# Moments of attention rows on ScalarE, the scan's skip term on TensorE, and a re-paced start of the experts in a fused state-space, attention and mixture-of-experts kernel

## The chip, the cores and the metric

The kernel runs on one core of a Trainium2 chip. The metric is the device time of one execution in microseconds. Before the change, three runs took 3665.78, 3655.67 and 3658.45 us; the median is 3658.45 us. One more execution was recorded with the hardware profiler.

## The reference

The input is four images of 384 channels and 32 x 32 places (1,024 tokens each), float32 throughout. Two layers follow each other:

```python
# layer 0: a selective scan over four directions k, 16 states n, after a group norm u = gn(x)
dt = softplus(dts + dt_bias)
h = h * exp(dt * A) + (dt * u) * B        # step by step along the 1,024 places
y = sum_n h * C  (+ Ds * u)               # summed over the four directions
x = x + gelu(layernorm_c(y) * ln_w + ln_b)
# layer 1, on tokens t = x transposed
t = t + softmax(causal(q k^T * scale)) v  # q, k, v from ln(t)
t = t + sum over the 2 best of 4 experts of  p_e * (gelu(ln(t) w1_e + b1_e) w2_e + b2_e)
```

`Ds * u` is the skip term. `ln(t)` in front of the experts needs the mean and the variance of each attention output row of 384 numbers.

## The kernel before

**The scan.** The work of layer 0 is cut into 768 units: 4 images x 3 channel blocks m of 128 x 4 directions x 16 units of 128 partitions (32 channels x 4 states) by 1,024 places. For a unit, `decay` (ScalarE) makes `da = exp(dt * a)`, `front` (VectorE, L709) the product `v = du * B` into PSUM, `middle` (VectorE, L715) the scan `h` from `da` and `v`, `back` (GpSimd, L732) the product of `h` with C. After every four units, `row` (L757) has TensorE sum the states of four h tiles into `y`, a PSUM tile of one block of channels. In the first image part of the `v` comes from TensorE and ScalarE instead (`feed`, `turned`). h has seven buffers; `ahead` makes VectorE wait, at each fourth unit, until the row sums of the four units before are done.

**Planner.** The program is written out by a loop over ticks `t`, one unit per tick. In every tick it emits the scan's instructions and then lets other work go on, which is written as generators: `preparation` of the next image, and on the list `waiting` the attention and the experts of the image before. A generator yields `("wait", n)`, to be taken up again n ticks later, or `("pe", x)`, which charges x us of TensorE to the budget of the tick: `PACE_A` 4.4 in attention, `PACE_E` 3.1 in the experts. All engines run their instructions in the order in which this loop emits them. `defer(n, f)` emits f n ticks later. `slots` are eight shared SBUF buffers, `banks` the shared PSUM banks; both are given back in the planner's time, and semaphores hold the engines to it. What is left after the last unit, the attention and experts of the fourth image (`alone`), runs by itself.

**Around the change.** `skip` (L765) loads `xe`, the normalised input of a block, when the last direction begins; `evict` (L773), two ticks after the last row sum of the block, adds `dsum * xe` to `y` and writes `yb` (L777); with the third block the image's layer norm begins (`finish`). In `attention`, `values` (L1225) sums an output row block of 128 tokens into the bank `po`; its inner `rows` (L1240) takes the moments with two VectorE instructions (L1242, L1243), copies the rows to `yb` on ScalarE and gives the bank back. `ready` (L1296) turns moments into `rstd` and `shift` and normalises the rows. `chosen` (L1368) ranks the experts, places the tokens, and sends each row block with two indirect DMAs of GpSimd's queue to its places in `xsd` (`scatter`, L1491); it adds to `routed` when they are emitted. `experts` (L1604) waits for all of `routed` (L1835), loads the first 256 rows (`load(0)`), turns them with TensorE, and goes through 11 blocks: `first_` (L1720) is 6 steps of 2 x 3 matmuls of w1 tiles (L1740), `second_` (L1774) 6 steps of matmuls of w2 tiles (L1790). Each step charges `PART` = 2.6 us (x `STEP`, which is 3 in the last image). `need` and `weights` fetch the weight tiles (384 KB each) up to four ahead. Blocks are filled by the data: `by_rows` branches to 256, 128 or no rows.

Of the kernel before, what the change touches and what calls it, by code (L numbers as in the profile page):

```python
# [9 lines left out]
F32 = mybir.dt.float32  # L10
# [7 lines left out]
P = 128  # L18
# [29 lines left out]
PACE_E = 3.1  # L48
PACE_T = 1.5
PART = 2.6  # L50
BT = 256
LIMIT = 44.0
EDGE = 40.0
# [5 lines left out]
def hybrid_kernel(  # L59
# [131 lines left out]
    def act(dst, src, f, **more):  # L191

        if f in KINDS:
            tables_for(KINDS[f])
        return nc.scalar.activation(dst, src, f, **more)  # L195
# [569 lines left out]
    def skip(b, m):  # L765
        xe = yield from slots.take(f"xe_{b}_{m}", P, L)
        nc.sync.dma_start(xe, xn_d[b][:, m, :])
        xes[b, m] = xe

    ybs = {}  # L770
    held = []
# [1 line left out]
    def evict(b, m):  # L773
        if m == 0:
            assert not held, f"tick {clock[0]}: the image before still needs the buffer"
            ybs[b] = one.tile([P, M, L], F32, tag="yb", name=f"yb_{b}")
        nc.vector.scalar_tensor_tensor(  # L777
            ybs[b][:, m, :], xes[b, m], dsum[:, m : m + 1], ys[b, m], ALU.mult, ALU.add
        )
        slots.give(f"xe_{b}_{m}")  # L780
        if m == M - 1:
            held.append(b)
            side.append(finish(b))
            waiting.append(behind(b))
# [322 lines left out]
    def attention(b, yb, fx0):  # L1107
# [117 lines left out]
        def values(i):  # L1225
            name = f"po_{b}_{i}"
            po = yield from banks.take(name)
            s = bass.ts(i, P)
            for m in range(M):
                nc.tensor.matmul(  # L1230
                    po[:, m * P : (m + 1) * P], yb[:, m, s], ident, start=(m == 0), stop=False
                )
            for j in range(i + 1):
                nc.tensor.matmul(  # L1234
                    po[:, :C], pts[i][:, j, :], vt[:, j, :], start=False, stop=(j == i)
                )
            yield "pe", 1.2 + 0.65 * (i + 1)
            slots.give(f"pt_{b}_{i}")

            def rows():  # L1240
                stat = sm.tile([P, 6], F32, tag="stat", name=f"stat_{b}_{i}")
                nc.vector.bn_stats(stat, po[:, :C])  # L1242
                nc.vector.bn_aggr(moments[:, i, :], stat)  # L1243
                nc.scalar.copy(yb[:, :, s], po[:, :C].rearrange("p (m t) -> p m t", m=M))
                banks.give(name)

                def kept():
                    nc.sync.dma_start(
                        t2_d[b][s, :].rearrange("p (m t) -> p m t", m=M), yb[:, :, s]
                    )  # L1250

                if alone:
                    kept()
                else:
                    defer(2, kept)
                for h, (q0, n) in enumerate(GROUPS):
                    if i == q0 + n - 1:
                        defer(1, lambda h=h, q0=q0, n=n: side.append(
                            ready(b, h, yb, group_rows(q0, n), moments)
                        ))  # L1260

            defer(1, rows, inner)
# [33 lines left out]
    def ready(b, h, yb, rows, moments):  # L1296

        alone = b == B - 1
        name = f"{b}_{h}"
        q0, n = GROUPS[h]  # L1300
        mean = moments[:, q0 : q0 + n, 0]
        rstd = small("rstd", name, 1, n)[:, 0, :]
        shift = small("shift", name, 1, n)[:, 0, :]
        act(rstd, moments[:, q0 : q0 + n, 1], AF.Sqrt, bias=eps)
        yield "wait", 1
        nc.vector.reciprocal(rstd, rstd)
        nc.vector.scalar_tensor_tensor(shift, mean, -1.0, rstd, ALU.mult, ALU.mult)
        yield "wait", 1
        for q in range(n):
            act(  # L1310
                rows[q].rearrange("p (m t) -> p m t", m=M), yb[:, :, bass.ts(q0 + q, P)],
                AF.Identity, bias=shift[:, q : q + 1], scale=rstd[:, q : q + 1],
            )
            if q % 2:
                yield "wait", 1
        if h == LAST:
            held.clear()
        xts = {}
        for q in range(n):
            if q % 2 == 0:  # L1320
                xt = yield from slots.take(f"xt_{name}_{q}", P, 2, C)
            ps = yield from banks.take(f"pxt_{name}_{q}")
            for m in range(M):
                nc.tensor.transpose(
                    ps[:, m * P : (m + 1) * P], rows[q][:, m * P : (m + 1) * P], ident
                )
            yield "pe", 0.5

            def put(q=q, ps=ps, xt=xt):
                nc.scalar.copy(xt[:, q % 2, :], ps[:, :C])  # L1330
                banks.give(f"pxt_{name}_{q}")
                xts[q] = xt[:, q % 2, :]

            defer(1, put)
        while len(xts) < n:
            yield "wait", 1
        yield "wait", 1
        pg = yield from banks.take(f"pgate_{name}")
        for q in range(n):
            for c in range(M):  # L1340
                nc.tensor.matmul(
                    pg[:, q * E : (q + 1) * E], xts[q][:, c * P : (c + 1) * P], gw[:, c, :],
                    start=(c == 0), stop=(c == M - 1),
                )
        if h == LAST:
            gated.add(b)
        yield "pe", 0.65 * n
        slots.give(*[f"xt_{name}_{q}" for q in range(0, n, 2)])
        yield "wait", 1
        groups = GROUPS if alone else WIDE  # L1350
        g = [i for i, (g0, gn) in enumerate(groups) if g0 <= q0 < g0 + gn][0]
        g0, gn = groups[g]
        if (b, g) not in raw:
            raw[b, g] = small("sc", f"{b}_{g}", gn, E), []
        sc, whole = raw[b, g]
        nc.vector.tensor_tensor(
            sc[:, q0 - g0 : q0 - g0 + n], pg[:, : n * E].rearrange("p (q e) -> p q e", e=E),
            gb.unsqueeze(1).to_broadcast([P, n, E]), ALU.add,
        )
        banks.give(f"pgate_{name}")  # L1360
        whole.extend(rows)
        if len(whole) < gn:
            return
        yield from chosen(b, g, sc, whole)
# [3 lines left out]
    def chosen(b, h, sc, rows):  # L1368
# [63 lines left out]
        cum = choice()  # L1432
        if not alone:
            slots.give(f"cmp_{name}")
        yield "wait", 1
        while h > 0 and (b, h - 1) not in counted:
            yield "wait", 1
        counted.add((b, h))
# [52 lines left out]
        def scatter(q):  # L1491
            for i in range(2):
                nc.gpsimd.indirect_dma_start(  # L1493
                    out=views[2 * (q0 + q) + i],
                    out_offset=bass.IndirectOffsetOnAxis(
                        ap=placed[:, q0 + q, i : i + 1], axis=0
                    ),
                    in_=rows[q], in_offset=None,
                )

        if alone:
            yield "wait", 1
            for q in range(n):
                scatter(q)
            routed.add((b, h))
            probabilities()
            kept()
            yield "wait", 1
        mts = []
        for part in parts:  # L1510
# [7 lines left out]
            yield "wait", 1  # L1518
            nc.scalar.copy(mt[:, : len(part) * P], pm[:E, : len(part) * P])
            banks.give(f"pm_{name}_{part[0]}")  # L1520
        if not alone:
            for q in range(n):
                scatter(q)
                if q < n - 1:
                    yield "wait", 1
            routed.add((b, h))
        nc.vector.tensor_tensor(
            two, at.unsqueeze(1).to_broadcast([P, 2, E, n]),
            spot.rearrange("p q i -> p i q").unsqueeze(2).to_broadcast([P, 2, E, n]), ALU.is_equal,
# [74 lines left out]
    def experts(b, route):  # L1604
# [62 lines left out]
        def load(j):  # L1667
            look_up(j)
            got[j] = yield from slots.take(f"xg_{b}_{j}", P, BT // P, C)
            nc.sync.dma_start(got[j], rows_of(xs_d[0], j))  # L1670
# [29 lines left out]
        def count_rows():  # L1700
            code = nc.tensor.value_load(
                tables[b][0:1, 2 * NBLK : 2 * NBLK + 1], min_val=0, max_val=4 ** NBLK - 1
            )
            for j in range(NBLK):
                filled[j] = (code >> (2 * j)) & 3
# [14 lines left out]
        def first_(j):  # L1720
# [4 lines left out]
            for f0 in range(0, NF, 2 * STEP):  # L1725
# [36 lines left out]

                for f, t, w, name, ps in parts:
                    defer(1, lambda f=f, ps=ps, name=name: moved(f, ps, name))
                yield "pe", PART * STEP

            def gelu():
                flat = ht.rearrange("p f t -> p (f t)")
# [5 lines left out]
        def second_(j, gone):  # L1774
            pss = {}
            for c0 in range(0, 6, STEP):
# [23 lines left out]

                by_rows(j, run, fill)
                slots.give(*[tiles["2", j, c][1] for c in range(c0, c0 + STEP)])
                yield "pe", PART * STEP
            yt = yield from slots.take(f"yt_{b}_{j}", P, 2, C)

            def out_():
# [23 lines left out]
        while alone and fetched[0] < 4:  # L1830
            while not slots.ready():
                yield "wait", 1
            weights()
        groups = GROUPS if alone else WIDE
        while not all((b, h) in routed for h in range(len(groups))):  # L1835
            yield "wait", 1
        yield from load(0)
        count_rows()
        yield "wait", 1
        yield from turn_(0)  # L1840
# [360 lines left out]
```

## Time and profile before

| what | us |
|---|---|
| median of three runs | 3658.45 |
| profiled execution | 3662.96 |
| its span, first to last instruction | 3661.3 |
| VectorE (DVE) busy | 2910.7 (79%) |
| TensorE (PE) busy | 2874.7 (79%) |
| ScalarE (ACT) busy | 2057.0 (56%) |
| GpSimd (POOL) busy | 1978.7 (54%) |
| mean granted TensorE clock | 0.857 |

The longest groups on GpSimd and TensorE:

```profile
L732 POOL TENSOR_TENSOR h<-h,bc 128x1024 f32<-128x1024 f32 x768 | 1817.3, 2370 | 1136.7 <-DVE v L709 963.2 <-PE y L757 45.5 <-DVE h L715 26.8
L757 PE MATMUL y<-h,sel 128*32 128x512 f32 x3072 | 624.0, 712 | 241.7 <-POOL h L732 214.4
L1740 PE MATMUL ph<-turned,w 128*128 128x256 f32 (+1 forms) x2568 | 543.3, 367 | 43.8 <-DMA w<-in_w 37.9 <-ACT ht L195 6.0
L1790 PE MATMUL py<-w,ht 128*128 128x384 f32 x1416 | 489.2, 495 | 22.5 <-DMA w<-in_w 22.4
```

A group has its line, engine, operation, names, shapes and count; then its busy time in us and the mean of one in ns; then the idle time of the engine just before such instructions, and what ended most of it. Matmuls of float32 stand in the trace as two records each. Line 195 is the helper `act`, so that ScalarE's activations share that line and are told apart by names. A row of 40 digits gives the busy share of 40 equal slices of the span in tenths (9 is 90% or more). A window line has the stretch, its length, then busy time and count of PE, PEld (weight loads), DVE, ACT and POOL, and at the end the granted clock, the DMA share and GB/s. A timeline line has start, length, engine, line, operation, and in brackets the idle time before it with what ended it.

### The profile page before, as it was taken

The page shows a single profiled execution, that of the slowest core. Times are in us where ns is not written, and L with a number is a line of the kernel's source. Part 1 is how long each engine was busy: PE and PEld are TensorE (multiplying, and loading weights), DVE is VectorE, ACT ScalarE, POOL GpSimd, SP SyncE. Part 2 cuts the span into 40 slices and gives each one's busy share as a digit, 9 for nine tenths or more (in the row PEclk, how much of TensorE's full clock was granted, in tenths as well). Part 3 has the DMA queues.
Part 4 walks back from the last instruction along what each step waited for, and adds up shares of the span by engine and source line. Part 5 has one row for each costly group of instructions (what it writes and reads, how often), then busy time and mean ns, then how long its engine had stood idle before and what let it go on. Part 6 is the DMA issues. An engine that isn't in the chain of part 4 may idle for free.

```text
span 3661.3 us, 42695 instructions
## 1 busy us (share of the span) xinstructions
PE 2874.7 (79%) x12934; PEld 1681.1 (46%) x12934; DVE 2910.7 (79%) x2205; ACT 2057.0 (56%) x3258; POOL 1978.7 (54%) x950
## 2 busy tenths in 40 slices
PE   4666676778499899669669897678499995789998
PEld 1333333344155555244246562235166651566775
DVE  6998899989979899998989999989989997220000
ACT  4888888556466666457556665446356664232221
POOL 3777677645646566755655666755656666010001
PEclk7677777789599999789689998789699997889997
DMA  6677666445468888555468888553487876125665
GB/s 191 230 261 264 213 222 221 178 161 201 163 227 300 306 295 298 197 193 172 160 238 292 307 306 292 189 179 125 145 302 276 306 271 214 41 67 173 199 197 158
DMA packets 405251, 799.21 MB, mean 218 GB/s; under 512 B 47500, under 2 KB 278620, under 8 KB 404972
## 3 DMA queue, kind: packets, MB, share of 16 engines
q1 hardware_dynamic: 390572, 770.01, 60.6%
q0 software_dynamic: 8192, 25.17, 2.1%
q8 instruction: 165, 2.70, 0.3%
q10 hardware_dynamic: 6208, 0.39, 0.1%
q14 instruction: 114, 0.93, 0.1%
HBM read 680.44 MB, written 115.02 MB: 217 GB/s over the span
## 4 chain that ended last, share of the span: by engine, by line
DVE 27%; PE 22%; DMA 3%; ACT 3%; issue 2%; POOL 1%; SPq 1%; another core or an unknown queue 0%; DVEq 0%; POOLq 0%; ACTq 0%
DVE h L715 15%; DVE v L709 9%; PE ph L1740 5%; PE py L1790 3%; PE v_end L1790 2%; DMA w<-in_w 1%; PE y_end L1790 1%; PE y L757 1%; PE pq L1133 1%; PE pv L1144 1%; PE y_end L1740 1%; PE v_end L1740 1%; ACT ht L195 1%; POOL h L732 1%; DMA dts<-dt 1%
## 5 line engine op out<-in xcount | busy, mean ns | idle before, releaser
L732 POOL TENSOR_TENSOR h<-h,bc 128x1024 f32<-128x1024 f32 x768 | 1817.3, 2370 | 1136.7 <-DVE v L709 963.2
L715 DVE TENSOR_TENSOR_SCAN h<-da,v 128x1024 f32<-128x1024 f32 x768 | 1749.2, 2283 | 69.2 <-PE v L1021 33.8
L195 ACT ACTIVATE da<-dt,a 128x1024 f32<-128x1024 f32 x768 | 882.9, 1160 | 773.6 <-DVE h L715 626.5
L709 DVE TENSOR_TENSOR v<-du,bc 128x1024 f32<-128x1024 f32 x664 | 861.2, 1297 | 90.9 <-PE y L757 44.4
L757 PE MATMUL y<-h,sel 128*32 128x512 f32 x3072 | 624.0, 712 | 241.7 <-POOL h L732 214.4
L1740 PE MATMUL ph<-turned,w 128*128 128x256 f32 (+1 forms) x2568 | 543.3, 367 | 43.8 <-DMA w<-in_w 37.9
L1740 PEld LDWEIGHTS ph<-turned,w 128*128 128x128 f32 x2568 | 455.5, 194 | 137.7 <-issue 42.7
L1790 PE MATMUL py<-w,ht 128*128 128x384 f32 x1416 | 489.2, 495 | 22.5 <-DMA w<-in_w 22.4
L757 PEld LDWEIGHTS y<-h,sel 128*32 128x32 f32 x3072 | 111.2, 119 | 614.6 <-POOL h L732 371.8
L1790 PEld LDWEIGHTS py<-w,ht 128*128 128x128 f32 x1416 | 265.0, 191 | 238.8 <-issue 40.1
L195 ACT ACTIVATE ht<-ph,b1t 128x256 f32<-128x256 f32 x470 | 196.0, 471 | 244.7 <-PE ph L1740 220.7
L1855 POOL DMA_INDIRECT g<-ysd,places x64 | 83.6, 1307 | 341.5 <-DMA ysd<-yt 325.7
L195 ACT ACTIVATE st<-turn,bt 128x128 f32<-128x128 f32 x832 | 243.2, 544 | 0.0
L1021 PE MATMUL v<-ident,st 128*128 128x128 f32 x832 | 154.6, 348 | 98.5 <-DVE h L715 88.8
L1021 PEld LDWEIGHTS v<-ident,st 128*128 128x128 f32 x832 | 127.1, 181 | 146.4 <-DVE h L715 83.6
L185 ACT ACT_TABLE_LOAD x122 | 156.5, 1283 | 13.0 <-issue 10.8
L565 PE MATMUL pdt<-xd,wdt 12*128 12x512 f32 x184 | 109.1, 742 | 27.1 <-ACT dt L195 12.9
L1493 POOL DMA_INDIRECT xsd<-fx,places x32 | 38.3, 1196 | 141.4 <-issue 139.1
L1809 DVE COPY yt<-y_end 128x384 f32<-128x384 f32 x3 | 1.7, 557 | 127.7 <-ACT ht L195 59.9
L1234 PE MATMUL po<-vt,pt 128*128 128x384 f32 x234 | 87.7, 523 | 6.6 <-ACT pt L1124 6.5
L195 ACT ACTIVATE ht<-ht 128x3072 f32<-128x3072 f32 x33 | 91.3, 2766 | 0.4
L1163 PE MATMUL ss<-axn,qt 128*128 128x512 f32 (+3 forms) x240 | 86.5, 501 | 2.0 <-ACT pt L1124 1.2
(424 smaller groups left out, 2669.1 us busy)
## 6 DMA issues: line engine op xcount, KB each, us to landing
w<-in_w SPq DMA_DIRECT2D x528, 384.0 KB
bc<-rows SPq DMA_DIRECT2D x384, 512.0 KB
dt<-dts SPq DMA_DIRECT2D x192, 512.0 KB
du<-dts SPq DMA_DIRECT2D x192, 512.0 KB
dts<-dt SPq DMA_DIRECT2D x48, 512.0 KB
dts<-du SPq DMA_DIRECT2D x48, 512.0 KB
xg<-xsd SPq DMA_DIRECT2D x44, 384.0 KB
ysd<-yt SPq DMA_DIRECT2D x44, 384.0 KB
```

The lines of the kernel that those rows point to most:

```text
L185: nc.scalar.preload_act_table_set(kind)
L195: return nc.scalar.activation(dst, src, f, **more)
L565: nc.tensor.matmul(pss[i], wdt[r, m * P : (m + 1) * P], xd[r, bass.ts(h, 512)], start=True, stop=True,)
L709: return nc.vector.tensor_tensor(u["v"], spread["du4", n], spread["bc", n][:, 0, :], ALU.mult)
L715: nc.vector.tensor_tensor_scan(u["h"][:, ::step], u["da"][:, ::step], u["v"][:, ::step], 0.0, op0=ALU.mult, op1=ALU.add,)
L732: product = units[n]["product"] = nc.gpsimd.tensor_tensor(h, h, spread["bc", n][:, 1, :], ALU.mult)
L757: units[n]["row"] = nc.tensor.matmul(y, sel, h, start=first, stop=last, tile_position=(0, jj * DJ))
L1021: nc.tensor.transpose(u["v"][:, t * P : (t + 1) * P], st[:, t, u["j"] * P : (u["j"] + 1) * P], ident)
L1163: nc.tensor.matmul(ps[:, : e - o], qt[:, c, i * P : (i + 1) * P], xn[o // 512][:, c, : e - o], start=(c == 0), stop=(c == M - 1 and (alone ...
L1234: nc.tensor.matmul(po[:, :C], pts[i][:, j, :], vt[:, j, :], start=False, stop=(j == i))
L1740: nc.tensor.matmul(ps[:, i * BT : i * BT + n], t[:, c, i * P : (i + 1) * P], xt[:, c, :n], start=(c == 0), stop=(c == M - 1),)
L1790: nc.tensor.matmul(pss[i][:, :C], hts[j][:, 2 * c + f, i * P : (i + 1) * P], tiles["2", j, c][0][:, f, :], start=(c == 0 and f == 0), stop ...
```

## The change

In `skip`, ScalarE makes a diagonal matrix `dg` from the identity and `dsum`, and TensorE adds `dg * xe` to `y` with two matmuls, before the last row sums; the slot of `xe` is given back there. `evict` only copies `y` to `yb`: on ScalarE, in the last image on VectorE. In `rows`, all images but the last have ScalarE make the moments: an Identity with a running sum while it copies the rows, a scaling of the sum to minus the mean, and a Square with a running sum, written back to the bank; `ready` takes the signs and the scale by C into account. In `chosen`, the scatters are emitted before the gates' transposes in all images (they came after them in all but the last), and one wait in front of the placing matmuls is two ticks. In `experts`, all images but the last charge 2.4 us a step, fetch up to three weight tiles while they wait for the routing, and wait two ticks before and two after the first load of rows.

```diff
+PACED = 2.4
...
     def skip(b, m):
         xe = yield from slots.take(f"xe_{b}_{m}", P, L)
         nc.sync.dma_start(xe, xn_d[b][:, m, :])
-        xes[b, m] = xe
+        yield "wait", 2
+        dg = one.tile([P, NH, P], F32, tag=f"rs{NH}", name=f"dg_{b}_{m}")[:, 0, :]
+        act(dg, ident, AF.Copy, scale=dsum[:, m : m + 1])
+        yield "wait", 1
+        for half in range(NH):
+            s = bass.ts(half, 512)
+            nc.tensor.matmul(ys[b, m][:, s], dg, xe[:, s], start=False, stop=False)
+            yield "pe", 1.0
+        slots.give(f"xe_{b}_{m}")
+        xes[b, m] = True
...
-        nc.vector.scalar_tensor_tensor(
-            ybs[b][:, m, :], xes[b, m], dsum[:, m : m + 1], ys[b, m], ALU.mult, ALU.add
-        )
-        slots.give(f"xe_{b}_{m}")
+        assert xes[b, m]
+        if b == B - 1:
+            nc.vector.tensor_copy(ybs[b][:, m, :], ys[b, m])
+        else:
+            nc.scalar.copy(ybs[b][:, m, :], ys[b, m])
...
             def rows():
-                stat = sm.tile([P, 6], F32, tag="stat", name=f"stat_{b}_{i}")
-                nc.vector.bn_stats(stat, po[:, :C])
-                nc.vector.bn_aggr(moments[:, i, :], stat)
-                nc.scalar.copy(yb[:, :, s], po[:, :C].rearrange("p (m t) -> p m t", m=M))
+                whole = po[:, :C].rearrange("p (m t) -> p m t", m=M)
+                if alone:
+                    stat = sm.tile([P, 6], F32, tag="stat", name=f"stat_{b}_{i}")
+                    nc.vector.bn_stats(stat, po[:, :C])
+                    nc.vector.bn_aggr(moments[:, i, :], stat)
+                    nc.scalar.copy(yb[:, :, s], whole)
+                else:
+                    mean, dev = moments[:, i, 0:1], moments[:, i, 1:2]
+                    act(yb[:, :, s], whole, AF.Identity, accum_out=mean)
+                    act(mean, mean, AF.Copy, scale=-1.0 / C)
+                    act(po[:, :C], po[:, :C], AF.Square, bias=mean, accum_out=dev)
                 banks.give(name)
...
         cum = choice()
         if not alone:
             slots.give(f"cmp_{name}")
-        yield "wait", 1
+        yield "wait", 1 if alone else 2
...
+        yield "wait", 1
+        for q in range(n):
+            scatter(q)
+            if not alone and q < n - 1:
+                yield "wait", 1
+        routed.add((b, h))
         if alone:
-            yield "wait", 1
-            for q in range(n):
-                scatter(q)
-            routed.add((b, h))
             probabilities()
...
-        if not alone:
-            for q in range(n):
-                scatter(q)
-                if q < n - 1:
-                    yield "wait", 1
-            routed.add((b, h))
...
-                yield "pe", PART * STEP
+                yield "pe", (PART if alone else PACED) * STEP
...
-                yield "pe", PART * STEP
+                yield "pe", (PART if alone else PACED) * STEP
...
+        begun = clock[0]
         groups = GROUPS if alone else WIDE
         while not all((b, h) in routed for h in range(len(groups))):
-            yield "wait", 1
+            if not alone and clock[0] >= begun + 2 and fetched[0] < 3 and slots.ready(1 + slots.kept):
+                weights()
+            yield "wait", 1
+        if not alone:
+            yield "wait", 2
         yield from load(0)
+        if not alone:
+            yield "wait", 2
         count_rows()
```

More of the change, by code (lines that the diff above doesn't have):

```diff
@@ L1303, in ready @@
         shift = small("shift", name, 1, n)[:, 0, :]
-        act(rstd, moments[:, q0 : q0 + n, 1], AF.Sqrt, bias=eps)
+        act(
+            rstd, moments[:, q0 : q0 + n, 1], AF.Sqrt, bias=eps, scale=1.0 if alone else 1.0 / C
+        )
         yield "wait", 1
         nc.vector.reciprocal(rstd, rstd)
-        nc.vector.scalar_tensor_tensor(shift, mean, -1.0, rstd, ALU.mult, ALU.mult)
+        nc.vector.scalar_tensor_tensor(
+            shift, mean, -1.0 if alone else 1.0, rstd, ALU.mult, ALU.mult
+        )
         yield "wait", 1
```

## The prediction

> **What bounds the kernel now.** I read the page's row of busy tenths first, then the groups, then the timeline of VectorE round one moved instruction, then the waits.
>
> ```profile
> PE   4666676778499899669669897678499995789998
> DVE  6998899989979899998989999989989997220000
> ```
>
> Read the two rows together: up to slice 34 (some 3,100 us) VectorE is at eight or nine tenths; after it VectorE is almost idle and TensorE works on what is left, the last image. So there are two programs in one: 768 scan units that VectorE paces, and a tail of 575 us (last scan's end at 3,086 us to the span's 3661.3 us), which TensorE and a chain of small steps pace. A change is worth something where it shortens a unit, or takes away a wait of VectorE before 3,086 us.
>
> ```profile
> L715 DVE TENSOR_TENSOR_SCAN h<-da,v 128x1024 f32<-128x1024 f32 x768 | 1749.2, 2283 | 69.2 <-PE v L1021 33.8 <-ACT da L195 5.8 <-POOL h L732 1.3
> L709 DVE TENSOR_TENSOR v<-du,bc 128x1024 f32<-128x1024 f32 x664 | 861.2, 1297 | 90.9 <-PE y L757 44.4 <-DMA du<-dts 14.8 <-ACT da L195 10.8
> L777 DVE SCALAR_TENSOR_TENSOR yb<-xe,dsum,y 128x1024 f32<-128x1024 f32 x12 | 15.2, 1269 | 5.1 <-PE y L757 5.1
> L1242 DVE BATCH_NORM_STATS2 stat<-po 128x6 f32<-128x384 f32 x27 | 15.0, 556 | 1.4 <-PE po L1234 1.4
> ```
>
> One unit is a product (1.26 us) and a scan (2.28 us). The last two rows are work that the change takes off VectorE. What one costs is not its duration but how much later the next scan starts:
>
> ```profile
> 2535.75 1.32 DVE L709 TENSOR_TENSOR v<-du,bc 128x1024 f32<-128x1024 f32 x1
> 2536.99 0.55 DVE L1242 BATCH_NORM_STATS2 stat<-po 128x6 f32<-128x384 f32 x1
> 2537.57 0.18 DVE L1243 BATCH_NORM_AGGREGATE moments<-stat 128x2 f32<-128x6 f32 x1
> 2537.67 2.25 DVE L715 TENSOR_TENSOR_SCAN h<-da,v 128x1024 f32<-128x1024 f32 x1
> ```
>
> The scan before started at 2533.43, so this unit took 4.24 us. Over the whole trace, the median from one scan's start to the next is 3.62 us where nothing else stands between, 4.18 us with the moments alone, 4.68 us with the skip's add of L777. The instructions overlap a little at their ends, so the gain is 0.56 and 1.06 us, not 0.74 and 1.27.
>
> **Part 1: VectorE's work.** 24 pairs of moments go (8 rows of three images; the last keeps them): 24 x 0.56 = 13.4 us. Nine adds of L777 become ScalarE copies: 9 x 1.06 = 9.5 us. The last image's three become a VectorE copy of the same 1,024 elements: nothing. Together 23 us. Six of the moments (scan units 223 to 229, 421 and 423) stand where VectorE also waits for attention's matmuls and bank copies; there the wait grows instead (-3.4). Two adds fall in the first image, where half of the unit's products come from TensorE (-1). I take 18 us; the ends are 12 and 23.
>
> **Part 2: what ScalarE takes over.** Per row an Identity and a Square of 384 elements from PSUM, each with a read of its accumulator, and a scaling of one column, for one copy: the copy is 0.48 us, the softmax's exponent of 512 with its accumulator 0.68 + 0.19, the square root of a few elements 0.30. So 2 x (0.55 + 0.19) + 0.25 - 0.48 = 1.25 us, x 24 = 30 us; nine copies of 1,024 at about 1.05 (squares of that size) 9.5; twelve scaled identities at 0.39, 4.7: 44 us on an engine that is busy 56%. The rows fall in some 90 us per image:
>
> ```profile
> 823.00:913.00 90.00, 78.39 (x339) 43.25 (x340) 85.70 (x89) 56.15 (x87) 48.09 (x22) 0.91 0.55 197
> ```
>
> ScalarE is the fourth pair: 56 of 90 us, and 66 with the added 10. The decays are issued two units ahead, so this hides; behind each triple wait only copies of attention and the next decay, 1.25 us later. The Trainium skill ("ScalarE: Activation LUTs", Rules for kernel authors) speaks against it: simple arithmetic belongs on VectorE. By that rule the part costs 30 us for 13; by the rows the 30 lie on an engine with 34 us free in this window. The row decides: 0. Without that cover it would be at most 30.
>
> **Part 3: TensorE's skip term.** 24 matmuls of 128x512, which stand in the trace as two rows each; the mean's L800 has the same shape (48 rows in 26.1 us), so 2.2 us per block of a channel third, 26 us in all. xe comes 11 us before its use, by the program's waits of three units. Seven blocks fall where TensorE has slack; those in expert stretches are counted in part 5.
>
> **Part 4: the start of the experts.** This is the largest wait that VectorE has:
>
> ```profile
> 1010.64 7.33 PE L1740 MATMUL ph<-turned,w 128*128 128x256 f32 x24 [10.69 <-DMA w<-in_w]
> 1025.26 1.23 DVE L709 TENSOR_TENSOR v<-du,bc 128x1024 f32<-128x1024 f32 x1 [10.36 <-PE y L757]
> ```
>
> TensorE stood 10.7 us before the first weights, with the scan's row sums (L757) queued behind; VectorE, which reuses their h buffers, then stood 10.4 us. With its after-effects (5.1 at 1067, 4.5 before L507) that is 20 us; the second image's start has 8.6 us of such gaps from 1858 to 1887, the third's 5.8 at 2672. The change sends up to three weight tiles while it waits for the routing, and puts two units (7 us) before and two after the first load of rows. I take 17 + 6 + 5 = 28 us; the ends are 8 (the first matmuls only find another late thing) and 34. The moved scatters are the same 16 per image, one pair per unit, in nearly the same units; they cost what they did.
>
> **Part 5: the quicker pace.** PACED 2.4 for 2.6 pays for the four added units: an expert step is charged less, so more are laid into a unit. What does TensorE have left?
>
> ```profile
> 2696.00:2824.00 128.00, 127.67 (x577) 83.23 (x576) 123.79 (x70) 81.94 (x105) 82.12 (x35) 1.00 0.83 289
> ```
>
> The first pair is TensorE, 127.67 of 128 us. The skill ("Perfetto Trace Analysis", Identifying the Most-Contended Engine) says that matmul busy time does not measure headroom and asks for the weight loads' share: 83 of 128, so 35% free, and the pace would cost nothing. But the rows stand end to end (24 of L1740 in 5.2 us, 0.216 each; 24 of L1790 in 7.8, 0.324). A full pair of block steps is 72 x 0.216 + 48 x 0.324 + 1.3 for the turned rows = 32.4 us, and each unit adds a quarter of 1.9 us of row sums. Planned before: (12 x 2.6 + 0.9)/3.1 = 10.35 units, TensorE 37.3 us, VectorE 37.5: just even. Planned after: (12 x 2.4 + 0.9)/3.1 = 9.58 units, 36.9 against 34.7: 2.2 us too much per full pair. So here the row decides against the rule. TensorE may be late by about two units less a row, 5.3 us, before VectorE stands, and half-filled blocks give it back. The trace shows which are full: the third image's experts six in a row, 6 x 2.2 - 5.3 = 8 us; the second's twice four, 2 x (8.8 - 5.3) = 7, and 3 for bursts, since VectorE already lost 9.9 us there between 1890 and 2200; the first's are full, full, half, 0, and 3 for bursts and the skip matmuls. 21 us lost; the ends are 5 and 53 (all 24 full pairs at 2.2).
>
> **The tail** keeps its instructions on every engine, but for the copy in place of L777 and six skip matmuls that come before it. The image before ends its experts about four units earlier, which nothing waits for: 0, with some us of scatter.
>
> **Sum.** -18 - 28 + 21 = -25 us. The profiled execution took 3662.96 us (span 3661.3), 4.5 more than the runs' median of 3658.45; from that median, **3633 us**.
>
> **Rivals.** (a) *TensorE becomes the bound* in the expert stretches: every full pair pays its 2.2 us at once (53), and the starts give 20: -18 - 20 + 53 = +15, 3673 us. It decides once the overload passes 46 us. For it: TensorE's 127.67 of 128. Against it: half-filled blocks and the lateness it is allowed. (b) *The start is late for another reason*, the rows' load or the copies: -18 - 8 + 21 = -5, 3653 us, no change. For it: pxg waited 51.4 us in total for xg. Against: the added units are as long as those waits. (c) *TensorE absorbs the pace*: -18 - 28 + 5 = -41, 3617 us; for it, its queue ran ahead of GpSimd's products for 21 us between 2690 and 2960. That the change leaves work where it was is excluded: the instruction order has 24 moments fewer.
>
> **How the numbers follow.** Forecast 0.50, (a) 0.16, (b) 0.16, (c) 0.18. The range 3606 to 3670 takes in (b), (c) and most of what lies before (a). A measurement tells 0.3%, 11 us, from no change. Faster: 0.46 + 0.18 + 0.03 = 0.67; same: 0.04 + 0.11 + 0.02 = 0.17; slower: 0.16.
>
> **What would show it.** The gaps at the three expert starts gone; plain units still 3.62 us; units with row moments down to that; new waits of L709 for TensorE's row sums in the third image's full stretch, some 8 us; the tail within a few us of 575. Wrong: those waits beyond 46 us in all, or decays late in attention.

## The result, and the profile after

The changed kernel took **3627.86 us** (median of four runs, 3624.53 to 3634.82), the kernel before 3658.36 us beside it: a ratio of 0.9917, 95% interval 0.9904 to 0.9929. The change makes the kernel faster by 0.8%, 30 us; 25 us were forecast. The profiled execution of the changed kernel took 3634.82 us, with a span of 3633.1 us against 3661.3.

First the two rows of busy tenths of the page after, for TensorE and VectorE:

```profile
PE   4666676778599999679589996678499985889998
DVE  6998888998999999989998999999999997130000
```

The picture is the same: VectorE paces the units up to slice 34, TensorE the tail. The last scan now ends at 3054.7 us instead of 3086.0; the tail is 578.4 us instead of 575.3. The whole gain lies in the units. These are the groups of the changed kernel that answer to those shown of before:

```profile
L716 DVE TENSOR_TENSOR_SCAN h<-da,v 128x1024 f32<-128x1024 f32 x768 | 1749.9, 2284 | 75.6 <-PE v L1032 38.3 <-ACT da L196 6.8 <-POOL h L733 1.0
L710 DVE TENSOR_TENSOR v<-du,bc 128x1024 f32<-128x1024 f32 x664 | 863.3, 1300 | 80.3 <-PE y L758 35.4 <-DMA du<-dts 18.0 <-DMA bc<-rows 4.7
L789 DVE COPY yb<-y 128x1024 f32<-128x1024 f32 x3 | 3.6, 1215 | 5.2 <-PE y L758 5.2
L196 ACT ACTIVATE po<-po,moments 128x384 f32<-128x384 f32 x24 | 13.3, 555 | 0.8
L196 ACT ACTIVATE yb<-po 128x384 f32<-128x384 f32 x24 | 11.9, 496 | 0.0
```

Scan and product last as long as before. The products' wait for row sums went from 44.4 to 35.4 us only, and their wait for `du` rose from 14.8 to 18.0. The longest wait for row sums fell from 10.4 to 6.2 us, while their number rose from 15 to 18: large waits went, and small ones came. A plain unit is still 3.62 us in both traces.

The first start of the experts, in the timeline of TensorE, begins in the changed kernel like this:

```profile
1022.68 5.34 PE L1758 MATMUL ph<-turned,w 128*128 128x256 f32 x24
1029.81 2.86 PE L1758 MATMUL ph<-turned,w 128*128 128x256 f32 x12
```

No bracket, so no wait: the matmuls that stood 10.69 us before their weights now start 12 us later, and find them. The next table tells where the time went, by stretches from scan to scan of the two traces of the comparison:

| stretch | after minus before, us |
|---|---|
| three starts of the experts (units 256-287, 448-479, 640-671) | -20.8, -10.0, -10.3 |
| first image's experts, units 320-351 (a 7.4 us wait behind a late weight is gone) | -9.5 |
| second image's experts, units 480-575 | +13.3 |
| third image's experts, units 672-703 | +3.7 |
| the three attention stretches (192-255, 384-447, 576-639) | -4.8 |
| all else, the first scan's start and the tail | +10.2 |
| span | -28.2 |

Repeated on another chip, each stretch of 32 units of the changed kernel from unit 192 on agrees within 1.5 us with this trace, two thirds of them within 0.3, so for this kernel a stretch tells more than a total does. The tail differs: 578 us on the first chip and 568 us on the second, which is most of what the two runs of the kernel differ by. The totals below are therefore compared as ratios to the kernel before on the same chip (3651 to 3653 us on those chips), and one thousandth is 3.65 us. By the intervals of the ratios, a difference between two kernels is known to some 6 to 8 us. Other kernels spread more than the changed one: its four runs on that chip lie within 4 us (10 on the first), those of the kernel with the moves of work alone within 13. The trace kept of a kernel is of one execution, and that need not be the middle one; where it lies far from the median and a reading rests on it, the text says so.

### The profile page after: what moved, and what is told of

Same layout as the page of the kernel before. It is cut to its first block, busy times and chain, and to the rows that moved or that the text cites. A ratio compares the mean times of both kernels' runs of the same rounds, so it can differ in the third digit from the quotient of the medians.

```text
span 3633.1 us, 42851 instructions
## 1 busy us (share of the span) xinstructions
PE 2902.2 (80%) x12982; PEld 1682.8 (46%) x12982; DVE 2898.7 (80%) x2148; ACT 2090.0 (58%) x3375; POOL 1982.5 (55%) x950
## 4 chain that ended last, share of the span: by engine, by line
PE 31%; DVE 27%; DMA 4%; issue 2%; ACT 2%; SPq 0%; POOL 0%; DVEq 0%; ACTq 0%; POOLq 0%
DVE h L716 14%; DVE v L710 9%; PE ph L1758 8%; PE py L1808 7%; PE y L758 2%; DMA w<-in_w 2%; PE v_end L1808 2%; PE y_end L1808 1%; PE pq L1144 1%; PE pv L1155 1%; PE y_end L1758 1%; PE v_end L1758 1%; ACT ht L196 1%; PE ss L1174 0%; PE pdt L566 0%
## 5 line engine op out<-in xcount | busy, mean ns | idle before, releaser
L710 DVE TENSOR_TENSOR v<-du,bc 128x1024 f32<-128x1024 f32 x664 | 863.3, 1300 | 80.3 <-PE y L758 35.4
L1758 PE MATMUL ph<-turned,w 128*128 128x256 f32 (+1 forms) x2568 | 534.8, 363 | 15.0 <-DMA w<-in_w 9.3
```

What stands on the lines that cost most here:

```text
L710: return nc.vector.tensor_tensor(u["v"], spread["du4", n], spread["bc", n][:, 0, :], ALU.mult)
L1758: nc.tensor.matmul(ps[:, i * BT : i * BT + n], t[:, c, i * P : (i + 1) * P], xt[:, c, :n], start=(c == 0), stop=(c == M - 1),)
```

## The experiments

### The two halves of the change

One kernel takes the moves of work alone, and one the schedule alone (summarised):

```diff
 offload_only: kernel before, and
+  skip on TensorE, evict on ScalarE, row moments on ScalarE
 schedule_only: kernel before, and
+  scatter order, weights during the routing, waits round load(0)
+  yield "pe", (PART if alone else PACED) * STEP      # PACED = 2.4
```

> The kernel before with the two moves of work alone: ScalarE makes the moments of the attention rows, TensorE adds the skip term, ScalarE copies the sums out. Pace 2.6, the scatters and the expert starts stay as they were. Theory (the forecast's sum): VectorE loses 18 us of work on its critical path and nothing else changes: 3640 us, 18 below before. Rival 1, the moves save nothing, because the freed moments turn into waits for TensorE or ScalarE: 3658. Rival 2, the whole of the change's 30 us comes from here and the schedule is neutral: 3628.

> The kernel before with the rest of the change alone: the scatters' order, the added waits, the weights sent while the routing is awaited, and pace 2.4. VectorE keeps the moments and the skip's addition. Theory (the forecast's terms): -28 at the starts and +21 by the pace, 3651 us. Reading of the trace of after, where the stretches of 8 units round the three starts are 24 + 10 + 12 us shorter and the second and third image's experts some 16 us longer: about 3630 to 3640. Rival, everything comes from the work taken off VectorE: 3658.

Measured: the moves of work **0.9995** (0.9987 to 1.0003), nothing to be seen, where 18 us were expected; the schedule **0.9983** (0.9977 to 0.999), -6 us, as the forecast's two terms have it (-28 + 21), and less than the reading of the trace had promised. Together that would be -8 us. The changed kernel on a third chip:

> The changed kernel once more, beside the others on one chip. Alone, the two moves of work gave 0.9995 of before and the schedule 0.9983. Theory A, the parts add: 0.9978. Theory B, each needs the other (the schedule's quicker pace loses in waits what the work taken off VectorE would win, or the freed moments are only worth something once the starts are gone): 0.992 as first measured, so some 20 us come from having both.

It gave **0.9904** (0.9888 to 0.992), 3617.8 us: -35 us. Theory B holds: some 27 us come only with both halves. Part of why the moves of work are worth nothing alone is seen at the starts of the experts. First the timeline of TensorE at the third start in the kernel before, then those of TensorE and VectorE in the kernel with these moves alone, at the first start and at the third:

```profile
2662.69 7.33 PE L1740 MATMUL ph<-turned,w 128*128 128x256 f32 x24 [6.74 <-DMA w<-in_w]
```

```profile
1009.06 8.28 PE L1762 MATMUL ph<-turned,w 128*128 128x256 f32 x24 [11.28 <-DMA w<-in_w]
...
1024.63 1.23 DVE L710 TENSOR_TENSOR v<-du,bc 128x1024 f32<-128x1024 f32 x1 [12.83 <-PE y L758]
...
2666.38 9.95 PE L1762 MATMUL ph<-turned,w 128*128 128x256 f32 x36 [11.74 <-DMA w<-in_w]
...
2678.53 1.23 DVE L710 TENSOR_TENSOR v<-du,bc 128x1024 f32<-128x1024 f32 x1 [7.49 <-PE y L758]
```

VectorE's wait at the first start is 12.83 us, where it was 10.36; TensorE's wait for weights at the third is 11.74, where it was 6.74, and VectorE's 7.49 for 5.81. VectorE comes sooner to a point that the weights set, and stands there longer. In this trace the units up to 639 are 14.6 us shorter than before, and the third start takes 4.8 of them back at once. That leaves 9.7 us in the units, while the totals show 2: the trace is of one of the quicker executions of this kernel (3645.81 us, the median is 3649.56), and that of before of a slow one (4.5 us above its median). So the starts explain 4 to 5 us; where the rest of the expected 18 went is not shown. The schedule alone has the gain at the starts (-19.8, -8.3 and -8.2 us in the same stretches) and loses 26 us in units 480 to 607.

### Each part taken back from the changed kernel

The edits below are cut to the lines that matter.

```diff
 no_moments: changed kernel, but in rows()
-  act(yb[:, :, s], whole, AF.Identity, accum_out=mean) ...
+  nc.vector.bn_stats(stat, po[:, :C]); nc.vector.bn_aggr(moments[:, i, :], stat)
 no_skip: changed kernel, but in evict()
-  nc.scalar.copy(ybs[b][:, m, :], ys[b, m])           # and the matmuls of skip()
+  nc.vector.scalar_tensor_tensor(ybs[b][:, m, :], xes[b, m], dsum[:, m : m + 1], ...)
+  slots.give(f"xe_{b}_{m}")
```

> The changed kernel with the row moments back on VectorE (statistics and aggregate, one ScalarE copy per row); skip term and schedule as changed. The forecast's term says +13 us on the changed kernel (24 x 0.56). If the moves of work save nothing here either: 0. If most of the 20 us that the parts lack come from ScalarE's moments: +20 or more.

> The changed kernel with the skip term back on VectorE (no matmuls, no ScalarE copies of the sums); moments and schedule as changed. The forecast's term says +9 us (9 x 1.06). Rival: the 26 us of matmuls that go from TensorE are worth more where the quicker pace overloads it, so that it is faster than the changed kernel, by up to 5 us.

Without ScalarE's moments: **0.9948** (0.9934 to 0.9962), 16 us slower than the changed kernel for the 13 expected. The traces put it where it should be: 3.5, 5.3 and 3.6 us in the three attention stretches, 12.4 us together. Without the skip move: **0.9974** (0.9966 to 0.9982), 26 us slower, where nine adds explain 9.5; the rival, that TensorE's relief makes it faster, is out. The 16 us left over were a surprise. Besides the adds, the matmuls and the copies, the move changes one thing: the moment at which `xe` gives its slot back. So:

```diff
 skip_hold: changed kernel, but
-        slots.give(f"xe_{b}_{m}")                      # in skip(), after the matmuls
+        slots.give(f"xe_{b}_{m}")                      # in evict(), some 14 units later
```

> The changed kernel, but the skip term's input keeps its SBUF slot until the sums are copied out, some 14 units longer, as it did in the kernel before; matmuls and copies as changed. Without the skip move the changed kernel lost 25 us where nine adds explain 9 or 10. Theory A, the slot: it holds back the weights of the experts, and the 15 us that are not explained are its price: 10 to 15 us slower than the changed kernel. Theory B, the 15 us come from VectorE's adds themselves, standing late in the expert stretches: 0.

**0.9949** (0.9935 to 0.9962), 16 us slower: theory A, just above its upper end. This kernel and the one without the skip move both hold the slot, and they differ by 9 us, which is what the nine adds come to. So 9 or 10 us for VectorE's adds and 16 for the slot make the 26. The waits of VectorE show what changes with the slot. First the changed kernel, then the one that holds the slot; the numbers are the total in us, how often, and the longest:

```profile
DVE v L710 <- PE y L758: 33.9, 15, 6.2
...
DVE v L710 <- DMA du<-dts: 18.6, 12, 3.8
```

```profile
DVE v L710 <- PE y L758: 49.4, 29, 6.2
...
DVE v L710 <- DMA du<-dts: 24.5, 13, 4.3
```

The row sums are late 29 times instead of 15, by 15.5 us more in total, with the same matmuls and the same VectorE work. (This trace is of the slowest of five executions, 3644.34 us for a median of 3635.16, so it shows somewhat more than the price of 16.) With one of eight slots missing for some 14 units in each block of channels, expert steps come to lie elsewhere in TensorE's order: between the row sums of four units, units 464 to 479 of the changed kernel hold five expert steps in each group; with the slot held they hold four, six, four and six. This bunching is not the whole mechanism, though. The kernel without the skip move holds the slot too, and has five steps in each of these groups; what the two have in common is that both lose 9 to 11 us in units 352 to 447, 6 to 7 in units 480 to 543 and 4 to 5 in units 576 to 607. The price of the slot is shown by the edit, which changes nothing else; how it acts, whether by weights, rows or outputs, which share the slots, stays open.

### The starts

```diff
 no_prefetch: changed kernel, but
-            if not alone and clock[0] >= begun + 2 and fetched[0] < 3 and slots.ready(1 + slots.kept):
-                weights()
 no_waits: changed kernel, but round load(0)
-        if not alone:
-            yield "wait", 2
 no_waits_26: the same, and
-PACED = 2.4
+PACED = 2.6
```

> The changed kernel without the weights sent while the routing is awaited; the two waits round the first load of rows, the scatters and the pace as changed. Theory A, the weights' head start takes the starts' waits away: 25 to 40 us slower, with TensorE waiting for in_w at each start again. Theory B, the added waits alone let VectorE run on while TensorE waits: under 10 us slower.

> The changed kernel without the two added waits of two units round the first load of rows; prefetch, scatters and pace as changed. Theory A: the rows are then asked for too early in TensorE's order, and TensorE waits for them with row sums behind it: 10 to 20 us slower at the three starts. Theory B: the waits only cost planned units, and with the weights there the starts are short anyway: 0, or faster, for the experts begin four units earlier and run as before.

> The changed kernel without the two added waits and with the old pace of 2.6: the two belong together, since with the waits and 2.6 the experts of an image end too late for the buffer of the next. Theory A: the overload of about 20 us goes, and the starts give back 10 to 20: within 10 us of the changed kernel. Theory B, the waits are worth nothing beside the prefetch: 15 to 20 us faster than the changed kernel, some 3600 us. Theory C, both matter: slower.

Without the early weights: **0.9977** (0.9965 to 0.9989), 27 us slower, within theory A's 25 to 40. (The trace is of one of the quicker executions and shows 22 of them.) Yet the loss is not at each start: at the first the stretch of 16 units is 63.3 us with and without them. It is at the second (10.6 us in units 464 to 479, of which 3.2 were gained in the 16 units before) and at the third (7.0 in units 656 to 671); the rest is scattered. TensorE at the third start without the early weights, and VectorE's answer:

```profile
2648.28 9.90 PE L1758 MATMUL ph<-turned,w 128*128 128x256 f32 x36 [7.25 <-DMA w<-in_w]
...
2657.61 1.23 DVE L710 TENSOR_TENSOR v<-du,bc 128x1024 f32<-128x1024 f32 x1 [2.37 <-ACT da L196]
2663.63 1.23 DVE L710 TENSOR_TENSOR v<-du,bc 128x1024 f32<-128x1024 f32 x1 [2.46 <-PE y L758]
```

That is before's wait of 6.74 us again. Without the added waits: **0.9999** (0.9991 to 1.0008), 35 us slower, so the whole gain goes; theory A had 10 to 20. 15.3 us of it are at the first start. There the trace without the waits shows the early weights in place and another thing late, the rows (first TensorE, then VectorE):

```profile
1005.47 1.51 PE L1697 MATMUL pxg<-ident,xg 128*128 128x128 f32 x6 [10.03 <-DMA xg<-xsd]
...
1042.11 1.22 DVE L508 TENSOR_REDUCE top<-xd 128x1 f32<-128x1024 f32 x1 [8.29 <-ACT xd L478]
1051.38 1.23 DVE L710 TENSOR_TENSOR v<-du,bc 128x1024 f32<-128x1024 f32 x1 [0.50 <-ACT da L196]
1062.41 1.23 DVE L710 TENSOR_TENSOR v<-du,bc 128x1024 f32<-128x1024 f32 x1 [3.81 <-PE y L758]
```

TensorE stands 10.03 us before it can turn the first rows (`pxg`), because their load has not landed. Behind that, matmuls of the next image's preparation (L474) alternate with the first expert steps, and VectorE's reduction L508 waits 8.29 us for their result `xd`. In the changed kernel TensorE has no such wait at the first start, and the same L508 starts with no wait. The early weights alone therefore leave the next late thing, the rows. TensorE's waits for them, in total, before, in the changed kernel, and without the added waits:

```profile
PE pxg L1679 <- DMA xg<-xsd: 51.4, 8, 25.6
PE pxg L1697 <- DMA xg<-xsd: 10.0, 3, 4.0
PE pxg L1697 <- DMA xg<-xsd: 29.3, 4, 11.8
```

So at the first start the four units of waiting put the experts behind their rows, their weights and the preparation; how the 15.3 us divide between the rows and the preparation was not separated. At the other two starts the weights' head start does the work: without the waits, units 448 to 479 and 640 to 671 take no more than 0.7 us longer than in the changed kernel, although TensorE stands 11.8 us for rows at the second; in this trace VectorE has no wait there.

The third kernel is the telling one: without the waits, but with the pace of 2.6, **0.9897** (0.9882 to 0.9913), the same as the changed kernel within the intervals, as theory A has it. **The waits and the quicker pace cancel.** Without the waits the pace of 2.4 costs 37 us; the waits give 35 back. The fourth combination, the waits with the pace of 2.6, has no time. It was expected at 3607 us, unless the experts would then end too late; they do: at tick 643 the fourth image's first sums need the buffer `yb`, which the image before still holds. What the pace of 2.4 costs beside the waits is therefore known only from the neighbouring paces.

### The pace

```diff
-PACED = 2.4
+PACED = 2.5      # and 2.2 in the other
```

> The changed kernel with a pace of 2.2 in place of 2.4. Theory: a full pair of block steps is planned over 0.77 units less, so TensorE is behind by 2.8 us more per pair, 5 in all, and with the full pairs that stand in a row in the second and third image (fourteen, less the lateness that is allowed) it costs 14 x 2.8 = 39 us more: about 3667 us. Rival, the pace is absorbed by half-filled blocks: 3628 to 3635.

> The changed kernel with a pace of 2.5 in place of 2.4. The plan of the experts is then 0.39 units, 1.4 us, longer per full pair of block steps. Theory: about half of the overload of 21 us goes: 10 us below the changed kernel. A pace of 2.2 cost 62 us by the trace's two ratios (1.0111 against 0.9917 to before), 31 per tenth, more than the 20 per tenth that was expected, so the gain may be up to 16. Rival, the overload at 2.4 is hidden: 0 to 3 us; or the experts end late and hold up the next image: slower.

A pace of 2.2 gave **1.0111** (1.0096 to 1.0126), slower than the kernel before and 76 us behind the changed one, where 39 were expected. VectorE's idle time over the last three images of units is 65 us more than in the changed kernel, but only 22 of that is its wait for row sums; the rest is for weights, `xd` and other things. A pace of 2.5 gave **0.9887** (0.987 to 0.9904). That is better than the changed kernel by 6 us in the ratios and by 4 in the medians on the same chip, with intervals that overlap, where 10 to 16 were expected; the totals do not tell the two apart. In its trace the second image's experts (units 480 to 543) are 11.6 us shorter, and 4.1 and 5.3 us are lost again at units 320 and 640, where the steps come to lie otherwise. The waits of VectorE with 2.5, against 33.9 and 18.6 us above:

```profile
DVE v L710 <- DMA du<-dts: 24.5, 15, 3.9
DVE v L710 <- PE y L758: 20.7, 9, 6.2
```

13 us of waits for row sums go with a tenth of the pace, and 6 us of waits for `du` come. So TensorE does not absorb all of the pace: the row sums do come late by it, though little of that reaches the total at this step. The overload cannot be read from TensorE's busy time. Here are windows of nearly equal length in the second image's experts, first of the changed kernel, then with 2.5 (busy us of TensorE, weight loads, VectorE, ScalarE, GpSimd):

```profile
1907.80:2037.00 129.20, 123.90 (x568) 77.74 (x567) 115.08 (x66) 83.06 (x109) 74.57 (x32) 0.99 0.79 275
```

```profile
1911.00:2040.00 129.00, 124.46 (x566) 77.51 (x565) 119.70 (x69) 86.19 (x112) 78.03 (x33) 0.99 0.83 294
```

TensorE and its weight loads are as busy in both, so neither share tells the overload. What differs is VectorE, 115 us against 120, and with it ScalarE and GpSimd by 3 us each.

### A pace for each image

```diff
-PACED = 2.4
+PACED = (2.4, 2.5, 2.6)
-        if not alone:
+        if b < 2:
             yield "wait", 2                            # at both places
-                yield "pe", (PART if alone else PACED) * STEP
+                yield "pe", (PART if alone else PACED[b]) * STEP
```

> The changed kernel with a pace for each image's experts: 2.4 for the first, 2.5 for the second, 2.6 for the third, and the two added waits at the first two starts only. Taken from the best stretch of each trace: the first image's experts as in the changed kernel (789.7 us from its first scan to the next image's), the second's as with a pace of 2.5 (796.5 for 807.1), the third's as without waits and with 2.6 (760.6 for 760.5). Theory A, stretches can be put together: 10 us faster than the changed kernel. Theory B, the third image's start falls on other units and waits for weights as before: no faster than the changed kernel.

3608.53 us (3608.03 to 3609.44), **0.9888** (0.9872 to 0.9905). By the medians that is 9 us below the changed kernel, by the ratios 6, with intervals that overlap; the trace's stretches are as theory A has them: 791.0, 797.1 and 761.5 us from image to image, where 789.7, 796.5 and 760.6 were put together. It is faster than the kernel before beyond doubt. That it is faster than the changed kernel is what the stretches say (4.8 and 5.1 us in units 480 to 543, 5.1 in units 672 to 735, and 5.7 lost at unit 640); the totals, taken on two chips, do not decide it.

## Why the prediction was right, and where it was not

**The total** is right: -30 us measured, -25 forecast. The way there is right in kind: work off VectorE and shorter starts gain, the quicker pace takes some back. That the number came so near is in part luck, for both gains were forecast too small, one gain was not seen at all, and the terms do not add up as the sum has them.

**Part 1, VectorE's work** (-18): somewhat too small. Taken back from the changed kernel, the moments are worth 16 us by the totals and 12.4 by the stretches, and the adds 9 or 10, near the full 13.4 and 9.5 of the plain count; whether the deduction of 3.4 for six moments beside attention's waits was due, these figures do not decide. What the part did not say is that this gain needs the other half of the change: alone it is worth 2 us, in part because VectorE then waits longer for the weights.

**Part 2, ScalarE** (0): right. A row now costs 0.50 + 0.20 + 0.20 + 0.56 + 0.19 = 1.65 us of ScalarE for 0.48, so 1.17 more for the 1.25 estimated. The same window of 90 us of the first image's attention, in the changed kernel:

```profile
823.00:913.00 90.00, 78.82 (x346) 43.96 (x346) 84.67 (x77) 66.97 (x123) 47.76 (x21) 0.92 0.53 184
```

ScalarE went from 56.15 to 66.97 us, as estimated, VectorE from 85.70 to 84.67 with twelve instructions fewer; the scans' wait for decays is 6.8 us in all, for 5.8. The rule of the Trainium skill ("ScalarE: Activation LUTs", Rules for kernel authors) that additions and multiplications go to VectorE and not to ScalarE would have cost some 16 us here, by the run without ScalarE's moments.

**Part 3, the skip term:** the matmuls are hidden, as said: of the two kernels that hold the slot, the one with the matmuls and the copies is the faster by 9 us, the whole of the adds. (TensorE's busy time rose by 27.5 us, 26 estimated; the matmuls' own rows are 35.1 us. And `xe` is not always there in time: TensorE stood 5.2 and 6.1 us for it in units 567 and 759.) But this is the step that failed most: it counted what the move adds and the add that it removes, and gave nothing for the slot that `xe` frees some 14 units earlier. That is worth 16 us in the finished kernel.

**Part 4, the starts** (-28): too small. The three stretches are 41 us shorter, of which 3 are adds of part 1, and 36 shorter with the schedule alone, both beyond the ends of 8 and 34; 9.5 more came at unit 320, where a late weight had held up a matmul that VectorE needed. The cause was half right. Late weights hold up the second and third starts. At the first, where the largest wait was, the early weights change nothing once the added waits are there; without these waits the rows come 10 us late. The moved scatters were put at 0. No run isolates them, but the schedule alone has the three attention stretches 9 us longer, of which 2.8 are in the first, where no quicker pace has come before; so what the scatters and the one longer wait cost stays open.

**Part 5, the pace** (+21): the sum is about right, the place is not. The traces show +13.3 us in the second image's experts and +3.7 in the third's, where 10 and 8 were forecast; these stretches hold all parts of the change, and no run takes the pace alone back to 2.6 beside the waits. That most of the 53 us is soaked up at 2.4 agrees with this. It no longer does at 2.2, which costs 76 us more: rival (a), TensorE as the bound, lies between the two, though the loss there is not TensorE's lateness alone. Rival (b) did not decide the total, but it was half right about the cause: the rows' load is late too, and the added waits are what covers it. Rival (c), that TensorE absorbs the pace, does not fit: without the waits the two tenths cost 37 us, and beside them one tenth changes the waits for row sums by 13.

**The balance** between parts 4 and 5 was argued wrongly in one respect: the forecast set the gain of the starts against the pace's loss as two independent terms. The runs show the added waits and the pace as one trade that is worth nothing (0.9897 without both, 0.9904 with both). What is left of the gain are the early weights (27), the slot (16), the moments (16) and the adds (9.5 by the count). These prices, each taken at the finished kernel, sum to 69 us where the whole is 35, so each part is worth more with the others in place; that they share slack of VectorE and TensorE is a likely reason, which no run shows.

## What to carry to other kernels

Where one engine waits at a fixed point for something that comes on its own clock, some of the work taken off that engine ahead of it goes into a longer wait, as at the third start here: take the wait away first, then count the work. When one late thing is fetched earlier, look for the next one behind it; here it was the rows behind the weights. When an operation moves to another engine, list the buffers that it holds and when they come free; an SBUF slot returned earlier was worth as much here as the instructions saved, or more (16 us, known to some 8, against 9.5). And a change that delays a start and then hurries to make up for it should be tried without both.

## What was not expected of the hardware

Stretches of the changed kernel's trace repeat to a few tenths of a us between executions, chips and even some other kernels: units 256 to 287 took 127.6 us in the changed kernel on both chips, and again without ScalarE's moments. Against this, three of its 18 stretches of 32 units from unit 192 on differ by some 1 us or more between its two traces, stretches before unit 192 by up to 5.5, and the runs of several other kernels spread over 13 to 17 us. So a difference of 2 us in a stretch can be read from single traces of a kernel whose runs agree, while the totals of several runs leave 6 to 8 us in doubt. And TensorE in the third image's full stretch is recorded as busy for the whole of 128 us both before and after (127.67 and 128.00), though the plan lays more steps into a unit after: from two such windows the record cannot tell which is overloaded.
